# Unread products on TensorE in planned gaps, and a fixed PSUM tile for the second conv

## The chip, the cores and the metric

The kernel runs on one core of one Trainium2 chip. The metric is the device time in microseconds of one execution, from the first to the last instruction of the slowest core (here the only one). Traces come from the hardware profiler; one traced execution is one sample of the same program.

Names used below: TensorE (PE) does matrix products and writes them to PSUM; VectorE (DVE), ScalarE (ACT) and GpSimd (POOL) are the other engines; SyncE (SP) only issues DMAs. "Granted clock" is the share of TensorE's full clock that the throttle let through, as the trace records it.

## The reference

Two layers on an input x of 32 images, 96 channels, 56 x 56 pixels, all float32.

```python
# layer 0: an inverted bottleneck with a residual
h = relu(bn(einsum('oc,bchw->bohw', w1, x)))      # 96 -> 576 channels, the first conv
h = relu(bn(depthwise3x3(h, wdw)))                # 576 channels, 9 taps each
x = x + bn(einsum('oc,bchw->bohw', w2, h))        # 576 -> 96, the second conv

# layer 1, on tokens t = (image, 3136 pixels, 96 channels)
h = relu(bn(einsum('bnc,hc->bnh', layernorm(t), w1)))     # 96 -> 192
X = fft(h, axis=1)                                        # over the 3136 tokens
xr = relu(X.real * rd - X.imag * idg + rb)
xi = relu(X.imag * rd + X.real * idg + ib)
t = t + bn(einsum('bnh,ch->bnc', real(ifft(xr + 1j * xi)), w2))
t = t + ffn(layernorm(t))     # 96 -> 384 -> 96, operands rounded to 8-bit floats, sums to 16-bit
```

The result goes back to the image layout. Batch norms are affine with given statistics, so they fold into weights and biases.

## The kernel before

**Tiling.** An image is done in two halves of 28 rows. The 576 hidden channels are four groups of 128 and one of 64. For each half and each group of 128, `unit` runs the first conv on TensorE (line L584, two products of 406 columns into one PSUM tile `ps`), evicts it on ScalarE with bias and relu (L594, into `hs`), and then does the nine depthwise taps: ScalarE begins the accumulator `acc` (L610) and makes one or two products (L626), VectorE adds six or seven taps (L637), and a DMA of GpSimd adds the products (L645). ScalarE ends with a relu (L654). The last 64 channels go through TensorE instead (`last_channels`: L686, L722, evicted at L705 and L751).

`front` does the second conv (L844, L878, with the residual as transposes of x and the shift as a product with ones at L860) into a PSUM tile of its own, `pw`, in two pieces of four and three groups of 112 pixels, each evicted on ScalarE (L891). It then normalises (L788 to L817), turns the tokens (L945), projects them to 192 (L963) and does the first step of the Fourier transform (L994), whose result goes through DRAM. `mid`, twice per image, does the second step, the weights and relu of the spectrum, the projection back to 96 and the first step of the inverse (L1073, L1102, L1108, L1117, L1159, L1171, L1198 to L1202). `back`, four times per image, does the last step (L1272), the norm, the quantised network (L1289, L1307, L1328, L1340 to L1352, L1369, L1378) and the residual (L1388, L1399, L1404).

Most float32 products stand in the trace as two records each, so a count of 14 is 7 products.

**What sets the order.** Nothing is ordered by hand. Each piece of work is a `Step` with an engine, a cost in microseconds, the steps before it, the buffers that it takes and gives back, and a rank, which says how early it is due. `Plan.emit` plays the whole program through with these costs: whenever an engine falls idle, the ready step of the least rank whose buffers are free is emitted. Each engine's queue is this order, and on the chip each engine works through its queue in order and waits on semaphores where an input isn't there yet. So a gap that the planner sees leaves no trace in the queue: it is just the time until the next instruction's semaphore comes.

The planner has a model of TensorE's throttle in `stretched`: [...]

[...] three `ps` tiles of two banks each, and one `pw` tile of two banks. `pw` is taken from its pool anew for each piece of a half image.

Of the kernel before, what the change touches and what calls it, by code (L numbers as in the profile page):

```python
# [32 lines left out]
F32 = mybir.dt.float32  # L33
# [8 lines left out]
C = 96  # L42
# [86 lines left out]
PACE = {"last": 3.023, "front": 0.4, "mid": 0.54, "back": 0.45}  # L129
CHAIN = 0.6  # L130

OFF = (-4.5, 0.5, 0.5, 8.5)
AT = (3.0, 0.5)

# [14 lines left out]
class Plan:  # L149
# [12 lines left out]
    def __init__(self, free):  # L162
        self.free = dict(free)
        self.steps = []
        self.now = self.pace = 0.0
        self.window, self.share, self.slow = 0, {}, False
        self.moving = []

    def stretched(self, now, work):

        at = now
        while work > 1e-9:
            w = int(at / self.WINDOW + 1e-9)
            while self.window < w:
                x = self.share.pop(self.window, 0.0) / self.WINDOW
                if x < self.LITTLE:
                    self.slow = True
                elif x >= self.FULL:
                    self.slow = False
                self.window += 1  # L180
            rate = 0.5 if self.slow else 1.0
            use = min(work / rate, max((w + 1) * self.WINDOW - at, 1e-6))
            self.share[w] = self.share.get(w, 0.0) + use
            at += use
            work -= use * rate
        return at - now

    def moved(self, now, moves):

# [21 lines left out]
    def emit(self):  # L211
        ready = {s.engine: [] for s in self.steps}
        idle = dict.fromkeys(ready, True)
        for s in self.steps:
            if not s.left:
                heapq.heappush(ready[s.engine], (s.rank, s.at, s))
        events, count, left = [(0.0, 0, None, None)], 1, len(self.steps)
        while events:
            now = events[0][0]
            while events and events[0][0] <= now:  # L220
                _, _, engine, s = heapq.heappop(events)
                if engine:
                    idle[engine] = True
                elif s:
                    for b in s.give:
                        self.free[b] += 1
                    for n in s.next:
                        n.left -= 1
                        if not n.left:
                            heapq.heappush(ready[n.engine], (n.rank, n.at, n))  # L230
            for engine, heap in ready.items():
                if not idle[engine]:
                    continue
                passed, wanted = [], set()
                while heap:
                    item = heapq.heappop(heap)
                    s = item[2]
                    short = {b for b in s.take if self.free[b] < s.take.count(b)}
                    if short or wanted.intersection(s.take):
                        wanted |= short  # L240
                        passed.append(item)
                        continue
                    for b in s.take:
                        self.free[b] -= 1
                    s.emit()
                    left -= 1
                    idle[engine] = False
                    cost = self.stretched(now, s.cost) if engine == "PE" else s.cost
                    late = self.moved(now, s.late) if isinstance(s.late, tuple) else s.late
                    heapq.heappush(events, (now + cost, count, engine, None))  # L250
                    heapq.heappush(events, (now + cost + late, count + 1, None, s))
                    count += 2
                    break
                for item in passed:
                    heapq.heappush(heap, item)
        assert not left, "a step waits for a buffer that nothing frees"


@with_exitstack
def tile_kernel(ctx: ExitStack, tc: tile.TileContext, d: dict, out: bass.AP):  # L260
    nc = tc.nc
# [4 lines left out]
    psa = ctx.enter_context(tc.tile_pool(name="psa", bufs=3, space=PSUM))  # L266
    psw = ctx.enter_context(tc.tile_pool(name="psw", bufs=1, space=PSUM))
    dram = ctx.enter_context(tc.tile_pool(name="scratch", bufs=2, space=DRAM))

    def psum():  # L270
        return psa.tile([128, 2, 512], F32, name="ps", tag="ps")
# [19 lines left out]
    ident = cst([128, 128], "ident")  # L291
# [124 lines left out]
    s = scale_of(vec[:, 0, :], vec[:, 3, :], 128, NK + 1)  # L416

    ps = psum()
    for k in range(NK + 1):
# [3 lines left out]
            lhsT=s[:, k : k + 1].to_broadcast([128, C]),  # L423
            rhs=ident,
            start=True,
            stop=True,
# [4 lines left out]
    s = scale_of(vec[:, 4, :], vec[:, 7, :], 128, NK + 1)  # L431
# [69 lines left out]
    def ffn():  # L501
# [6 lines left out]
        for o, v, p, n in ((b1q, fb, 128, 3), (b2q, fc, C, 1)):  # L508
# [9 lines left out]
    plan = Plan(  # L518
        {
            "ps": 3, "pw": 1, "hs": 3, "acc": 7, "product": 3, "hl0": 1, "hl1": 1, "al": 2,  # L520
            "xt": 1, "norma": 2, "brief": 3, "xnT": 1, "z": 2, "ya": 1, "wb": 1, "yb": 2,
            "V": 2, "eo": 3, "real": 1, "wd": 1, "gd": 1, "tt": 2, "normf": 2, "u8": 1, "uT": 1,
            "h8": 1, "h16": 2, "y16": 1, "ydr": 4, "gdr": 3, "tdr": 4,
        }
    )
# [19 lines left out]
    for n, (f, count) in enumerate(((second, 7), (attention, 6), (mixer, 21), (ffn, 4))):  # L545
        t = step("SP", 0.55 * count, fetch, sets[-1:], late=(150e3, 170e3, 1.5), rank=-20.0 + n)
# [279 lines left out]
    def front(img, s):  # L826

        plan.job(32 * img + 16 * (s + 1) + START["front"], PACE["front"])
        u = {}
        x0 = (R * s - base[s]) * S  # L830

        def conv(i):

            def f():
                if i == 0:
                    if s == 0:

                        ydr[img] = dram.tile([2, NP, S, HA], F32, name="ydr", bufs=4)

                        tdr[img] = dram.tile([2, SK, RP * C], F32, name="tdr", bufs=4)  # L840
                    u["t"] = w1.tile([SK, RP, C], F32, name="xt")

                def add(n, t, src, rhs, rows=slice(None), **k):
                    nc.tensor.matmul(  # L844
                        u["pw"][0:SK, t, n % 4, 0:C],
                        lhsT=src[rows, (G * t + n) * SK : (G * t + n + 1) * SK],
                        rhs=rhs,
                        skip_group_check=True,
                        **k,
                    )  # L850

                if i % 4 == 0:
                    u["pw"] = psw.tile([128, 2, 4, 128], F32, name="pw", tag="pw")
                    n = min(4, G - i)

                    for t in range(2):
                        for m in range(i, i + n):
                            src = xs[img, s][:, x0 : x0 + W]
                            add(m, t, src, ident[0:C, 0:C], start=(m == i), stop=False, is_transpose=True)
                        nc.tensor.matmul(  # L860
                            u["pw"][0:SK, t, 0:n, 0:C],
                            lhsT=ones,
                            rhs=shb[:, 0:n, :],
                            start=False,
                            stop=False,
                            skip_group_check=True,
                        )
                for t in range(2):
                    for k in range(NK):
                        src = acc[img, s, k].rearrange("p r c -> p (r c)")  # L870
                        add(i, t, src, w2T[:, k, :], start=False, stop=False)
                if i in (3, 6):

                    last = acc[img, s, NK].rearrange("p r c -> p (r c)")
                    for n in range(i - i % 4, i + 1):
                        for t in range(2):
                            rows = slice(64 * t, 64 * t + 64)
                            nc.tensor.matmul(  # L878
                                u["pw"][0:SK, t, n % 4, 0:C],
                                lhsT=last[rows, n * SK : (n + 1) * SK],  # L880
                                rhs=w2T[rows, NK, :],
                                start=False,
                                stop=True,
                                skip_group_check=True,
                            )

            return f
# [14 lines left out]
        t = [ready[img, s, k] for k in range(NK)] + [strips[img, s], second_set]  # L902
        ev = []
        for i in range(G):
            n = min(4, G - i) if i % 4 == 0 else 0
            cost = pe(C, SK, 16) + n * (pe(C, SK, 2) + 0.13)
# [12 lines left out]
            if i in (3, 6):  # L919
                a = i - i % 4  # L920
# [498 lines left out]
    for i in range(nimg):  # L1419
        for s in range(2):  # L1420
            load_half(i, s)
            last_channels(i, s)
            for k in range(NK):
                unit(i, s, k)
            front(i, s)
        for half in range(2):
            mid(i, half)
        for h in range(4):
            back(i, h)
    with tc.manual_schedule():  # L1430
        plan.emit()

# [61 lines left out]
```

## Time and profile before

| what | value |
|---|---|
| time, median of 3 runs | 4695.46 us (4678.52 to 4697.34) |
| span of the traced run | 4680.7 us |
| mean granted TensorE clock | 0.967 |
| TensorE busy | 4397.9 us, 94% |
| VectorE busy | 4299.8 us, 92% |
| ScalarE busy | 4170.2 us, 89% |
| taps on VectorE (L637) | 1664 of 1793 ns, 2971.6 us |
| second conv (L844) | 7168 records, 804.9 us |
| eviction of `pw` (L891) | 128 of 629 to 862 ns |

Busy time is the union of an engine's instructions. TensorE's products overlap in its pipeline, so a busy TensorE is not one at its peak, and weight loads stand in a row of their own. The granted clock is given for the whole run and for any stretch. In the rows of waits the numbers are microseconds in total, times, and the longest. The first tap starts at 23.6 us and the last at 4431.3 us. Before and after these there is no depthwise work, and what remains at the end is the chains of the last images' `mid` and `back`.

### The profile page before, as it was taken

The page shows a single profiled execution, that of the slowest core. Times are in us where ns is not written, and L with a number is a line of the kernel's source. Part 1 is how long each engine was busy: PE and PEld are TensorE (multiplying, and loading weights), DVE is VectorE, ACT ScalarE, POOL GpSimd, SP SyncE. Part 2 cuts the span into 40 slices and gives each one's busy share as a digit, 9 for nine tenths or more (in the row PEclk, how much of TensorE's full clock was granted, in tenths as well). Part 3 has the DMA queues.
Part 4 walks back from the last instruction along what each step waited for, and adds up shares of the span by engine and source line. Part 5 has one row for each costly group of instructions (what it writes and reads, how often), then busy time and mean ns, then how long its engine had stood idle before and what let it go on. Part 6 is the DMA issues. An engine that isn't in the chain of part 4 may idle for free.

```text
span 4680.7 us, 85686 instructions
## 1 busy us (share of the span) xinstructions
PE 4397.9 (94%) x33744; PEld 3205.3 (68%) x33744; DVE 4299.8 (92%) x6933; ACT 4170.2 (89%) x5510; POOL 337.3 (7%) x397
## 2 busy tenths in 40 slices
PE   7889999999999999999999999999999999999986
PEld 4567776676676767676777676676776776676774
DVE  8999999999999999999999999999999999999943
ACT  4777999999999999999999999998998999899976
POOL 0000000000000000000000000000000000000000
PEclk7999999999999999999999999999999999999987
DMA  4667777767776767776767777777776776777752
GB/s 97 135 158 172 183 179 171 178 167 171 178 175 166 186 163 185 177 181 167 180 170 176 183 176 169 181 176 171 184 182 166 181 179 163 184 178 175 170 135 78
DMA packets 390887, 789.28 MB, mean 169 GB/s; under 512 B 135600, under 2 KB 236532, under 8 KB 390484
## 3 DMA queue, kind: packets, MB, share of 16 engines
q1 hardware_dynamic: 335028, 479.15, 36.4%
q0 software_dynamic: 55296, 304.64, 33.6%
q8 instruction: 266, 4.36, 0.4%
q14 instruction: 137, 1.12, 0.1%
q10 hardware_dynamic: 160, 0.01, 0.0%
HBM read 286.38 MB, written 192.68 MB: 102 GB/s over the span
## 4 chain that ended last, share of the span: by engine, by line
PE 46%; ACT 14%; DVE 11%; DMA 6%; issue 2%; SPq 0%; POOLq 0%; ACTq 0%; DVEq 0%
PE pw L844 10%; PE ps L584 8%; DVE acc L637 7%; DMA acc<-product 5%; PE ps L722 4%; PE ps L1073 3%; PE ps L994 2%; PE ps L963 2%; PE ps L1369 2%; PE ps L1272 2%; PE ps L1171 2%; ACT acc L654 2%; PE ps L1328 2%; ACT product L626 1%; ACT acc L610 1%
## 5 line engine op out<-in xcount | busy, mean ns | idle before, releaser
L637 DVE SCALAR_TENSOR_TENSOR acc<-hs,wdw,acc 128x1540 f32<-128x1540 f32 (+2 forms) x1664 | 2971.6, 1793 | 27.2 <-ACT acc L610 18.6
L584 PE MATMUL ps<-xs,w1T 96*128 96x406 f32 x2048 | 823.4, 526 | 48.8 <-ACT al L751 11.6
L844 PEld LDWEIGHTS pw<-w2T,acc 128*112 128x112 f32 x7168 | 766.4, 181 | 64.3 <-issue 40.3
L844 PE MATMUL pw<-w2T,acc 128*112 128x96 f32 x7168 | 804.9, 267 | 5.0 <-ACT acc L654 4.8
L626 ACT ACTIVATE product<-hs,wdw 128x1568 f32<-128x1568 f32 (+1 forms) x384 | 609.4, 1591 | 14.5 <-DMA product<-product 14.1
L584 PEld LDWEIGHTS ps<-xs,w1T 96*128 96x128 f32 x2048 | 371.2, 195 | 300.0 <-issue 136.0
L594 ACT ACTIVATE hs<-ps,b 128x812 f32<-128x812 f32 x512 | 478.6, 935 | 97.8 <-PE ps L584 83.2
L645 POOL DMA_DIRECT2D acc<-product x256 | 227.7, 890 | 3306.4 <-DVE acc L637 384.9
L654 ACT ACTIVATE acc<-acc 128x1568 f32<-128x1568 f32 x256 | 386.9, 1512 | 63.8 <-DMA acc<-product 63.5
L610 ACT ACTIVATE acc<-hs,bd,wdw 128x1568 f32<-128x1568 f32 x256 | 435.2, 1700 | 5.5 <-DVE eo L498 5.4
L722 PE MATMUL ps<-hl,band 128*64 128x385 f32 (+3 forms) x3072 | 419.3, 498 | 4.5 <-ACT hs L594 2.3
L963 PE MATMUL ps<-watt,xnT 97*120 97x192 f32 x1792 | 350.3, 341 | 44.3 <-DVE V L1102 31.4
L963 PEld LDWEIGHTS ps<-watt,xnT 97*120 97x120 f32 x1792 | 305.2, 190 | 105.4 <-DVE V L1102 40.2
L1289 ACT ACTIVATE u<-tt,mf,rf 112x96 fp8e5<-112x96 f32 x896 | 346.4, 462 | 6.1 <-DVE mf L820 5.9
L1352 ACT ACTIVATE h<-h 128x784 fp8e5<-128x784 f16 x384 | 329.4, 860 | 22.3 <-DVE h L1346 21.1
L1073 PEld LDWEIGHTS ps<-wb,yb 112*128 112x128 f32 (+1 forms) x3584 | 306.9, 167 | 58.5 <-issue 23.9
L1340 ACT ACTIVATE h<-ps 128x784 f16<-128x784 f32 x384 | 315.4, 824 | 26.8 <-PE ps L1328 25.7
L1073 PE MATMUL ps<-wb,yb 112*128 112x112 f32 (+1 forms) x3584 | 330.7, 273 | 4.0 <-ACT hs L594 1.8
L722 PEld LDWEIGHTS ps<-hl,band 128*64 128x64 f32 (+1 forms) x3072 | 154.7, 135 | 204.1 <-issue 168.8
L1346 DVE TENSOR_SCALAR h<-h,b1q 128x784 f16<-128x784 f16 x384 | 160.8, 419 | 122.0 <-ACT h L1340 119.9
L994 PE MATMUL ps<-z,wa 56*64 56x384 f32 (+1 forms) x2048 | 242.6, 510 | 24.3 <-ACT hs L594 18.2
L1328 PE MATMUL ps<-uT,w1q 96*128 96x392 fp8e5 x768 | 196.9, 341 | 26.5 <-ACT xnT L948 9.5
(148 smaller groups left out, 6395.6 us busy)
## 6 DMA issues: line engine op xcount, KB each, us to landing
acc<-product POOLq DMA_DIRECT2D x256, 784.0 KB, 8.5
product<-product POOLq DMA_DIRECT2D x128, 756.0 KB, 10.7
yb<-ydr SPq DMA_DIRECT2D x256, 294.0 KB
wd<-in_wd_dram SPq DMA_DIRECT2D x128, 349.1 KB
wb<-in_wb_dram SPq DMA_DIRECT2D x64, 686.0 KB
ydr<-ya SPq DMA_DIRECT2D x256, 168.0 KB
xs<-in_x_dram SPq DMA_DIRECT2D x64, 609.0 KB
tdr<-xt SPq DMA_DIRECT2D x64, 588.0 KB
```

What stands on the lines that cost most here:

```text
L584: nc.tensor.matmul(u[h][:, j, 0:QW], lhsT=w1T[:, 128 * k : 128 * (k + 1)], rhs=xs[img, s][0:C, at : at + QW], start=True, stop=True,)
L594: nc.scalar.activation(flat[:, 2 * h * QW : 2 * (h + 1) * QW].rearrange("p (j w) -> p j w", j=2), u[h][:, :, 0:QW], AF.Relu, bias=b1[:, k ...
L610: nc.scalar.activation(acc[img, s, k], u["hs"][:, o + up : o + up + R, :], AF.Identity, scale=weight(up, 0), bias=bd[:, k : k + 1],)
L626: nc.scalar.activation(u["p", dr][:, ra:rb, :], u["hs"][:, ra + o + dr : rb + o + dr, :], AF.Copy, scale=weight(dr, 0))
L637: nc.vector.scalar_tensor_tensor(dst, src, weight(dr, dc), dst, ALU.mult, ALU.add)
L654: nc.scalar.activation(acc[img, s, k], acc[img, s, k], AF.Relu)
L722: nc.tensor.matmul(pv[:, :, ca:cb], lhsT=band[rows, j, dc + 1, 64 * o : 64 * o + 64], rhs=H[rows, q : q + 7, ca + dc : cb + dc], skip_grou ...
L844: nc.tensor.matmul(u["pw"][0:SK, t, n % 4, 0:C], lhsT=src[rows, (G * t + n) * SK : (G * t + n + 1) * SK], rhs=rhs, skip_group_check=True, **k,
L963: nc.tensor.matmul(pv[0:PK, q - a, 0:HA], lhsT=xnT[:, q, 0:PK], rhs=watt, start=True, stop=True,)
L994: nc.tensor.matmul(u["y", b][64 * c : 64 * c + n, j, 0 : 2 * HA], lhsT=wa[at, 0:n], rhs=rhs, start=True, stop=True)
L1073: nc.tensor.matmul(o, lhsT=lhsT, rhs=u["wb"][:, G * s + q, :], start=True, stop=True)
L1289: nc.scalar.activation(u["u8"][:, q, :], u["t"][:, q, :], AF.Identity, scale=u["r"][:, q : q + 1], bias=u["m"][:, q : q + 1], saturate=False,)
```

## The change

It does two things.

Where the planner finds TensorE idle with no step that it could start, and TensorE was used for less than three quarters (`SPARSE`) of the last window, it now emits a filler: a product of the 128 x 128 identity with itself, which nothing reads, for which the planner's clock moves on by 0.23 us (`FILLER`). When the planned filler ends, the planner looks again. Fillers stop when no TensorE step is left. [...]

For a place to put the filler's result, the `pw` tile becomes one fixed tile of two banks for the whole kernel. Its slots are 96 columns wide in place of 128, so that four of them leave the last 128 columns of each bank free; the filler writes into those of the first bank. One product before the plan opens the accumulation there.

```diff
--- before.py
+++ after.py
@@ -129,6 +129,9 @@
 PACE = {"last": 3.023, "front": 0.4, "mid": 0.54, "back": 0.45}
 CHAIN = 0.6
 
+SPARSE = 0.75
+FILLER = 0.23
+
 OFF = (-4.5, 0.5, 0.5, 8.5)
 AT = (3.0, 0.5)
 
@@ -165,6 +168,7 @@
         self.now = self.pace = 0.0
         self.window, self.share, self.slow = 0, {}, False
         self.moving = []
+        self.filler, self.recent = None, []
 
     def stretched(self, now, work):
 
@@ -185,6 +189,11 @@
             work -= use * rate
         return at - now
 
+    def sparse(self, now):
+
+        self.recent = [r for r in self.recent if r[1] > now - self.WINDOW]
+        return sum(b - max(a, now - self.WINDOW) for a, b in self.recent) < SPARSE * self.WINDOW
+
     def moved(self, now, moves):
 
         size, rate, extra = moves
@@ -215,6 +224,7 @@
             if not s.left:
                 heapq.heappush(ready[s.engine], (s.rank, s.at, s))
         events, count, left = [(0.0, 0, None, None)], 1, len(self.steps)
+        work = sum(s.engine == "PE" for s in self.steps)
         while events:
             now = events[0][0]
             while events and events[0][0] <= now:
@@ -246,6 +256,9 @@
                     left -= 1
                     idle[engine] = False
                     cost = self.stretched(now, s.cost) if engine == "PE" else s.cost
+                    if engine == "PE":
+                        self.recent.append((now, now + cost))
+                        work -= 1
                     late = self.moved(now, s.late) if isinstance(s.late, tuple) else s.late
                     heapq.heappush(events, (now + cost, count, engine, None))
                     heapq.heappush(events, (now + cost + late, count + 1, None, s))
@@ -253,6 +266,14 @@
                     break
                 for item in passed:
                     heapq.heappush(heap, item)
+                if engine == "PE" and idle[engine] and work and now > 0 and self.sparse(now):
+
+                    self.filler()
+                    idle[engine] = False
+                    cost = self.stretched(now, FILLER)
+                    self.recent.append((now, now + cost))
+                    heapq.heappush(events, (now + cost, count, engine, None))
+                    count += 1
         assert not left, "a step waits for a buffer that nothing frees"
 
 
@@ -266,6 +287,9 @@
     psa = ctx.enter_context(tc.tile_pool(name="psa", bufs=3, space=PSUM))
     psw = ctx.enter_context(tc.tile_pool(name="psw", bufs=1, space=PSUM))
     dram = ctx.enter_context(tc.tile_pool(name="scratch", bufs=2, space=DRAM))
+
+
+    pw = psw.tile([128, 2, 512], F32, name="pw", tag="pw")
 
     def psum():
         return psa.tile([128, 2, 512], F32, name="ps", tag="ps")
@@ -850,7 +874,7 @@
                     )
 
                 if i % 4 == 0:
-                    u["pw"] = psw.tile([128, 2, 4, 128], F32, name="pw", tag="pw")
+                    u["pw"] = pw[:, :, 0 : 4 * C].rearrange("p t (q c) -> p t q c", c=C)
                     n = min(4, G - i)
 
                     for t in range(2):
@@ -1427,6 +1451,12 @@
             mid(i, half)
         for h in range(4):
             back(i, h)
+
+    def filler():
+        nc.tensor.matmul(pw[:, 0, 4 * C :], lhsT=ident, rhs=ident, start=False, stop=False, skip_group_check=True)
+
+    nc.tensor.matmul(pw[:, 0, 4 * C :], lhsT=ident, rhs=ident, start=True, stop=False, skip_group_check=True)
+    plan.filler = filler
     with tc.manual_schedule():
         plan.emit()
```

## The prediction

> **What bounds the kernel now.** I read the page first for the shares of the engines, then the table of windows for three stages (start, steady state, end), then the chain of waits over the end, and last who waited for whom on TensorE. The page's parts 1 and 4:
>
> ```profile
> PE 4397.9 (94%) x33744; PEld 3205.3 (68%) x33744; DVE 4299.8 (92%) x6933; ACT 4170.2 (89%) x5510; POOL 337.3 (7%) x397
> ...
> PE 46%; ACT 14%; DVE 11%; DMA 6%; issue 2%; SPq 0%; POOLq 0%; ACTq 0%; DVEq 0%
> ```
>
> Three engines are each busy for about nine tenths of 4681 us, and TensorE has the largest part of the chain. No single engine can be named from this; the stages differ. The windows (busy us of PE, weight loads, DVE, ACT, POOL, then the granted TensorE clock and the DMA columns):
>
> ```profile
> 0.00:530.00 530.00, 454.37 (x3075) 318.84 (x3076) 484.04 (x613) 381.55 (x428) 45.76 (x63) 0.89 0.64 144
> 530.00:4430.00 3900.00, 3754.36 (x29375) 2739.06 (x29374) 3710.06 (x5971) 3610.98 (x4784) 290.71 (x334) 0.99 0.73 176
> 4430.00:4680.00 250.00, 189.18 (x1295) 147.42 (x1294) 105.66 (x351) 177.71 (x300) 0.86 (x1) 0.80 0.42 110
> ```
>
> The start is VectorE's (484 of 530 us busy), with a TensorE clock of 0.89. In the steady state TensorE is 96% busy, VectorE 95%, ScalarE 93%, and the clock is almost whole. In the last 250 us the depthwise taps are over: no engine is full, one image's chain runs after another, and the clock is 0.80. A low clock costs most where the chain is bare. The chain of waits over the end shows the same work twice (start us, us, what):
>
> ```profile
> 4559.13 1.38 PE ps L1272 x14
> ...
> 4616.07 2.60 PE ps L1272 x14
> ...
> 4652.60 2.69 PE ps L1272 x14
> ```
>
> and the windows beside two of them:
>
> ```profile
> 4480.00:4490.00 10.00, 6.04 (x60) 4.83 (x60) 6.51 (x13) 8.58 (x18) 0.00 (x0) 0.94 0.35 107
> 4490.00:4495.00 5.00, 4.75 (x21) 4.56 (x19) 2.91 (x4) 3.20 (x4) 0.00 (x0) 0.50 0.08 29
> ...
> 4650.00:4655.00 5.00, 4.70 (x21) 3.65 (x22) 0.00 (x0) 3.04 (x8) 0.00 (x0) 0.50 0.23 69
> ```
>
> A group of 7 products costs 1.38 us at the whole clock and 2.69 us where the granted clock is 0.50; a stretch in which TensorE was busy 6.04 of 10 us was enough to lose it.
>
> [...] 2.69 / 1.38 = 1.95, and the granted clock is 0.50 in the stretch. [...] between 4478 and 4492 the longest wait of TensorE was 2.5 us (line L945 for DVE xn L937), and the clock fell all the same. [...]
>
> **The change, part by part.** *Number and place of fillers.* The built instruction order has 961 fillers and one opening product, in 300 runs: 217 lie among the first four images' first-conv products (L584), 487 among those of the other 28, 257 after the last one. Apart from them, each engine has as many instructions as before, but the planner's interleaving has shifted everywhere, since a filler holds the planned TensorE for 0.23 us.
>
> *Price of one.* The trace has no warm 128x128 by 128 f32 product alone. From below: L1171, 7 products of 128x112 weights and 96 columns, takes 1.54 us on the chain (at 4472), 0.22 us each. From above: that times 128/112, 0.25 us. [...] I take 0.23: 50 us of TensorE at the start, 112 in the steady state, 59 at the end, 221 in all.
>
> *Clock lost before.* The mean clock is 0.967, so 0.033 x 4681 = 154 us of full clock were lost: 0.11 x 530 = 58 at the start, 0.20 x 250 = 50 at the end, and about 46 in the steady state.
>
> *Start.* VectorE idles 46 us of 530; about 8 of them lie in the first 20 us of loading and setup. The other 38 are dips at image borders, where TensorE has a burst of second conv and attention products to do and begins it at half clock after a gap. The 58 us can't return more than those 38. I take 15: ScalarE and DMA waits share the dips. Filler time costs nothing here, as TensorE idles 76 us (530 - 454) against 50 us of fillers.
>
> *Steady state.* The order puts the fillers once per image beside L963, L994, L1328, L1388 and L1307, 12 and 22 of them in alternate images. In the trace of before TensorE's waits there in this stage were
>
> ```profile
> PE ps L963 <- DVE V L1102: 31.4, 25, 2.6
> PE ps L994 <- ACT hs L594: 18.2, 20, 2.4
> PE ps L1328 <- ACT xnT L948: 9.5, 6, 2.2
> PE ps L1328 <- ACT z L976: 7.2, 2, 3.7
> PE ps L1388 <- DVE V L1102: 7.1, 10, 1.4
> ```
>
> 73 us, with L584 after ACT z (5.4) 79 us of the 146 that TensorE idles. So 112 - 79 = 33 us of fillers have no idle time to lie in and stand in front of real products, whose evictions (L594, L976) and taps queue behind them. Against that stand 46 us of lost clock, of which I count 0.6 on the path, the part that TensorE has in a chain nearly covered by engines (46 of 79%): 29 us. Net +4 us.
>
> *End.* I went down the chain from 4434 and took from each cold piece its warm twin: L963 twice 4.8 against 2.3, L1272 three times 2.6 to 2.7 against 1.38, L1159 three times 2.9 against 1.55, L1388 and L1369 some 0.5 too long each time. The excess comes to about 22 us. The fillers raise use from 181 of 240 us (some of it stretched) by 59 us, [...] I count nine tenths kept, 20 us. Some 30 runs lie on the chain and a product that becomes ready meets a running filler, half of 0.23 us each: 3.5 us back. Net -16.5.
>
> *The PSUM tile.* One fixed tile in place of one per half image, slots of 96 in place of 128: same bytes evicted, same number of products; the next conv waits for L891's eviction as it did. Three of the 961 fillers newly wait for ScalarE. Behind such a filler all of TensorE is queued. L844's longest wait for ACT xt was 1.8 us, so at most 5.4 us in all; hidden for the most part, as the filler stood in a gap: 0, upper bound 5.
>
> Sum: 4695.5 - 15 + 4 - 16.5 = **4668 us**.
>
> **The rivals.** *TensorE becomes the bound.* In the steady state the planned gaps need not be gaps on the chip: an order that is late on TensorE executes the fillers anyway, at once and without a wait. If half of the 79 us are met, 72 us of fillers displace work; with half of the 46 us recovered that is +49, with -6 at the start and -10 at the end: 4728 us. For it: 96% busy already, 146 us spare against 112 of fillers. Against: VectorE and ScalarE are as full, so a late TensorE is partly absorbed. *The clock isn't held.* Nothing paces the fillers on the chip: a run goes off back to back at the front of a gap and leaves the rest empty, [...]. Then a third of the gains at the ends (-10) and half the displacement (+5): 4690 us. For it: waits of 3.8 us in the end (L1369 for ACT h). *All of it returns.* Fillers lie in idle time alone, start -25, end -19, steady state -15: 4636 us.
>
> **How the numbers follow.** Forecast 0.48, TensorE bound 0.24, clock not held 0.18, all returns 0.10. The forecast spreads over some 15 us to each side, by the reordering alone; the bound of 0.5% is 4672 below and 4719 above. Faster: 0.30 of the forecast, 0.10, and 0.02 of "not held", 0.42. Slower: 0.21 of the TensorE case and 0.02 of the others, 0.23. Same: the remaining 0.35. Range 4636 to 4728: the two outer cases' times, which leave half of each outside, about 0.17; the price bounds of a filler (0.22 to 0.25) move the steady state by -5 to +10 and lie inside.
>
> **What would show it.** Right: the clock over the last 250 us above 0.9 and L1272 at 1.4 us throughout; the start's clock above 0.95, with fewer VectorE dips; 3900 us of steady state within 10 us. Wrong: a steady state longer by 20 us or more with TensorE above 98% busy (first rival); a clock in the end that stays near 0.8 with fillers in short bunches before idle time (second rival); or a time that moves while the clock does not, which would put it on the new interleaving.

## The result, and the profile after

The kernel after takes 4662.5 us (median of 4 runs, 4660.0 to 4665.7), the kernel before 4695.5 (median of 4, 4678.5 to 4697.3). The ratio of the means is 0.9938 with a 95% interval of 0.9914 to 0.9962: faster by 0.6%. The forecast was 4668.

The page of after, busy time by engine and the chain of waits by engine:

```profile
PE 4507.9 (97%) x35666; PEld 3363.0 (72%) x35666; DVE 4297.8 (92%) x6933; ACT 4177.0 (90%) x5510; POOL 339.8 (7%) x397
...
PE 60%; ACT 13%; DVE 13%; issue 3%; DMA 3%; SPq 0%; DVEq 0%; ACTq 0%; POOLq 0%
```

The chain of waits could be followed back to 360 us here and only to 928 us in before, and its shares are of the whole span. So TensorE's 60% here and 46% there don't compare as they stand.

TensorE has 1922 more records (two to a filler and to the opening product, 962 products; two records are missing) and is busy 110 us longer, in a span that is 22.5 us shorter. The same three windows as before (PE, weight loads, DVE, ACT, POOL, then the clock and the DMA columns):

```profile
0.00:530.00 530.00, 477.01 (x3432) 348.95 (x3432) 466.58 (x599) 367.53 (x409) 44.83 (x61) 0.94 0.63 141
530.00:4430.00 3900.00, 3828.37 (x30511) 2839.69 (x30511) 3734.05 (x6000) 3646.19 (x4826) 295.00 (x336) 1.00 0.74 177
4430.00:4658.00 228.00, 202.49 (x1725) 174.38 (x1724) 97.20 (x335) 163.25 (x279) 0.00 (x0) 0.97 0.41 111
```

The clock rose in all three: 0.89 to 0.94, 0.99 to 1.00, 0.80 to 0.97. In the start VectorE did less, not more: 466.6 us against 484.0. And the group of seven products that cost 2.6 to 2.7 us in the cold stretches of the end (clock 0.50; now line L1296) costs 1.38 to 1.63 us wherever the chain of waits has it after 4425 us, and 1.38 in its last five places, of which three are:

```profile
4580.11 1.38 PE ps L1296 x14
...
4607.24 1.38 PE ps L1296 x14
...
4634.27 1.38 PE ps L1296 x14
```

The waits of TensorE in the steady state (530 to 4430 us; total, times, longest):

```profile
PE ps L1412 <- DVE V L1126: 14.3, 25, 0.9
PE ps L1393 <- ACT xnT L972: 12.8, 12, 1.1
PE ps L987 <- DVE V L1126: 11.3, 16, 1.3
```

L987 is L963 of before, which waited 31.4 us there; 11.3 are left.

To see where the time went I cut each trace at three events instead of fixed times: the first depthwise tap, the 209th (image 5 begins; 52 taps to an image) and the last of 1664. All in us of the traced run, with "clock lost" as (1 - granted clock) times the stretch:

| | first tap | image 5 begins | image 5 to last tap | last tap to end | clock lost: start, middle, end |
|---|---|---|---|---|---|
| before | 23.6 | 508.7 | 3922.6 | 249.4 | 56, 46, 51 |
| after | 36.0 | 525.7 | 3885.1 | 247.3 | 31, 0, 8 |

The start got 17 us longer, the middle 37.5 us shorter, the end only 2 us shorter. The middle and the end of before, as the trace gives them (those of after stand below, beside the same order without fillers):

```profile
508.70:4431.30 3922.60, 3774.19 (x29517) 2754.36 (x29515) 3732.16 (x5993) 3633.33 (x4815) 293.08 (x336) 0.99 0.73 175
4431.30:4680.70 249.40, 188.23 (x1291) 146.81 (x1289) 104.36 (x350) 176.41 (x298) 0.86 (x1) 0.79 0.42 110
```

These are single traced runs; the kernel with the tile alone (below), whose order is that of before, has a middle of 3932.2 and an end of 247.0, so such numbers scatter by some 10 us in the middle and 2 in the end where the clock isn't held.

### The profile page after: what moved, and what is told of

Read it like the earlier page. It is cut to its first block, busy times and chain, and to the rows that moved or that the text cites. A ratio compares the mean times of both kernels' runs of the same rounds, so it can differ in the third digit from the quotient of the medians.

```text
span 4658.2 us, 89512 instructions
## 1 busy us (share of the span) xinstructions
PE 4507.9 (97%) x35666; PEld 3363.0 (72%) x35666; DVE 4297.8 (92%) x6933; ACT 4177.0 (90%) x5510; POOL 339.8 (7%) x397
## 4 chain that ended last, share of the span: by engine, by line
PE 60%; ACT 13%; DVE 13%; issue 3%; DMA 3%; SPq 0%; DVEq 0%; ACTq 0%; POOLq 0%
PE pw L868 15%; PE ps L608 10%; DVE acc L661 7%; PE ps L1097 4%; PE ps L1018 4%; PE ps L987 3%; PE ps L1296 3%; ACT product L650 2%; PE ps L1195 2%; PE ps L1352 2%; PE ps L746 2%; PE pw L902 2%; PE ps L710 2%; PE ps L1393 2%; PE ps L1183 2%
## 5 line engine op out<-in xcount | busy, mean ns | idle before, releaser
L608 PE MATMUL ps<-xs,w1T 96*128 96x406 f32 x2048 | 806.0, 516 | 18.4 <-ACT hs L618 13.5
L868 PEld LDWEIGHTS pw<-w2T,acc 128*112 128x112 f32 x7168 | 752.2, 179 | 64.7 <-issue 44.6
L650 ACT ACTIVATE product<-hs,wdw 128x1568 f32<-128x1568 f32 (+1 forms) x384 | 609.5, 1588 | 17.1 <-DMA product<-product 16.7
L987 PE MATMUL ps<-watt,xnT 97*120 97x192 f32 x1792 | 336.0, 331 | 15.0 <-DVE V L1126 12.3
L987 PEld LDWEIGHTS ps<-watt,xnT 97*120 97x120 f32 x1792 | 294.2, 184 | 69.7 <-issue 36.2
L1456 PE MATMUL pw<-ident 128*128 128x128 f32 x1920 | 276.8, 283 | 3.2 <-ACT xt L915 3.2
L1456 PEld LDWEIGHTS pw<-ident 128*128 128x128 f32 x1920 | 254.5, 196 | 25.8 <-issue 12.8
```

The lines of the kernel that those rows point to most:

```text
L608: nc.tensor.matmul(u[h][:, j, 0:QW], lhsT=w1T[:, 128 * k : 128 * (k + 1)], rhs=xs[img, s][0:C, at : at + QW], start=True, stop=True,)
L650: nc.scalar.activation(u["p", dr][:, ra:rb, :], u["hs"][:, ra + o + dr : rb + o + dr, :], AF.Copy, scale=weight(dr, 0))
L868: nc.tensor.matmul(u["pw"][0:SK, t, n % 4, 0:C], lhsT=src[rows, (G * t + n) * SK : (G * t + n + 1) * SK], rhs=rhs, skip_group_check=True, **k,
L987: nc.tensor.matmul(pv[0:PK, q - a, 0:HA], lhsT=xnT[:, q, 0:PK], rhs=watt, start=True, stop=True,)
L1456: nc.tensor.matmul(pw[:, 0, 4 * C :], lhsT=ident, rhs=ident, start=False, stop=False, skip_group_check=True)
```

## The experiments

Two theories. **The clock**: the fillers hold TensorE's clock, and that is the gain. **The interleaving**: a filler takes time in the plan, so every queue has a new order; the order is the gain, or part of it.

Edits are shown in part: `...` stands for what is left out, notes after `#` are mine, and `calls` counts the fillers that the plan has asked for.

**Planned, not emitted (e1).** The new order without one filler.

```diff
     def filler():
-        nc.tensor.matmul(pw[:, 0, 4 * C :], lhsT=ident, ...)
+        pass
```

> The order of after on every engine, with the fillers planned but not put into the queue. Theory 1 (the clock): the fillers hold the granted clock, and the gain in the steady state is theirs. Then the clock falls back to about 0.96 to 0.97, the depthwise stage (first tap to last tap, 4375 us in after, 4408 in before) grows back to 4395 or more, and the whole is 4680 to 4700 us. Theory 2 (the interleaving): the gain is the new order's, and fillers only cost. Then the stage stays at 4375 or shrinks, and the whole is 4640 to 4660 us although the clock is low.

Measured: 4707.0 us, ratio 1.0024 (1.0012 to 1.0036), a little over what theory 1 expected. Clock 0.962, clock lost 67, 58 and 53 us by stage. Its middle and end by its own events, and under them those of after:

```profile
528.30:4444.60 3916.30, 3784.78 (x29470) 2757.18 (x29469) 3732.29 (x5986) 3637.51 (x4805) 293.49 (x336) 0.99 0.74 175
4444.60:4699.50 254.90, 191.34 (x1334) 147.52 (x1332) 107.59 (x355) 178.94 (x303) 0.86 (x1) 0.79 0.42 111
```

```profile
525.70:4410.90 3885.20, 3818.08 (x30425) 2830.74 (x30424) 3727.88 (x5987) 3635.58 (x4805) 295.01 (x336) 1.00 0.74 177
4410.90:4658.20 247.30, 217.09 (x1847) 187.49 (x1844) 107.67 (x355) 178.16 (x303) 0.86 (x1) 0.97 0.43 115
```

The order alone is slower than before, by 0.2%. It costs most in the start: the first tap comes at 29.2 us and image 5 begins at 528.3, against 23.6 and 508.7. With the same order on every engine, the fillers take 31 us off the middle and 7.6 off the end. Theory 2 falls as the source of the gain; the order is a cost.

**The tile alone (e2).** Before, with one fixed `pw` and slots of 96, no fillers.

```diff
-                    u["pw"] = psw.tile([128, 2, 4, 128], F32, name="pw", tag="pw")
+                    u["pw"] = pw[:, :, 0 : 4 * C].rearrange("p t (q c) -> p t q c", c=C)
```

> The kernel before with only the fixed PSUM tile and slots of 96; no fillers, the same order on every engine. Both theories: no change, 4690 to 4700 us (ratio 0.997 to 1.003). If the tile were worth something, its eviction (629 to 862 ns in before) or the conv's waits would move and the ratio would be under 0.997.

Measured: 4694.5 us, ratio 1.0002 (0.9989 to 1.0015). The tile is worth nothing by itself, as forecast.

**The order of before, with fillers (e5).** In before's plan, with the fixed tile, ahead of each TensorE step, as many fillers as fit the planned gap less 0.85 us; they take no time in the plan.

```diff
+                    if engine == "PE":
+                        for _ in range(int(max(0.0, now - self.ended - 0.85) / 0.23)):
+                            self.filler()
                     s.emit()
```

> The order of before on every engine, with fillers put into the gaps that its own plan has on TensorE (as many as fill the gap less 0.85 us, at 0.23 us each: 553, of which 229 in the first four images, 161 in the others, 164 after the last first conv); they take no time in the plan. Fixed tile as in after. Theory 1 (the clock): clock 0.98 or more, depthwise stage 4380 to 4395 us, whole 4660 to 4680. Theory 2 (the interleaving): stage 4400 to 4420 us, whole 4690 to 4710 us although the clock rises.

Measured: 4671.5 us, ratio 0.9954 (0.9938 to 0.9971), clock 0.987. With the old order on every engine the fillers alone are a gain of 0.5%. Its 161 fillers in the middle left 20 us of clock lost there and the middle at 3914.3 us, 8 to 18 us under the two traces of this order without fillers, which themselves differ by 10 (I expected 4380 to 4395 us from first to last tap; it was 4404). The start got 4.5 us longer (image 5 begins at 513.2 us). The end is where it won:

```profile
4427.50:4662.90 235.40, 196.49 (x1619) 165.54 (x1617) 104.39 (x350) 175.12 (x298) 0.86 (x1) 0.95 0.44 117
```

235 us against 249 in before and 247 in after. So theory 1 holds on both orders, and the order of after has a worse end.

**The first 24 fillers (e3).** After, without the fillers that stand ahead of the first conv.

```diff
+        calls.append(0)
+        if len(calls) > 24:
             nc.tensor.matmul(...)
```

> The order of after, without the first 24 fillers alone, which stand ahead of the first conv and take 6.9 us there. In after the first tap starts at 36.0 us, in before at 23.6. If the time of these fillers makes the delay, the first tap comes at 24 to 29 us and the whole at 4650 to 4656. If it is the order that the plan made with them (the second norm's square root behind the first eviction on ScalarE, and its copies behind later loads), the first tap stays at 31 us or later, and the whole at 4657 to 4663.

Measured: 4653.0 us, ratio 0.9919 (0.9903 to 0.9935), first tap at 29.3 us: 6.7 of the 12.4 us of delay returned. Both causes are at work: the order without a filler has its first tap at 29.2 us, so 5.6 us of the delay are the order's and the rest is the 24 fillers'. The timelines show how. TensorE and then ScalarE in after (start us, us, engine, line, operation; in brackets the idle time before and what ended it):

```profile
7.83 6.86 PE L1456 MATMUL pw<-ident 128*128 128x128 f32 x48
14.53 5.63 PE L608 MATMUL ps<-xs,w1T 96*128 96x406 f32 x16
```

```profile
16.10 0.94 ACT L618 ACTIVATE hs<-ps,b 128x812 f32<-128x812 f32 x1 [11.97 <-PE ps L608]
16.94 0.27 ACT L430 ACTIVATE V<-V 128x96 f32<-128x96 f32 x1
30.09 2.35 ACTq L482 DMA_DIRECT2D shb<-yb  x3
32.49 1.77 ACT L618 ACTIVATE hs<-ps,b 128x812 f32<-128x812 f32 x2 [15.28 <-DMA shb<-yb]
```

and ScalarE in before:

```profile
10.85 0.28 ACT L406 ACTIVATE V<-V 128x96 f32<-128x96 f32 x1 [6.62 <-DVE V L405]
14.06 5.09 ACTq L458 DMA_DIRECT2D shb<-yb  x3
19.20 2.59 ACT L594 ACTIVATE hs<-ps,b 128x812 f32<-128x812 f32 x3 [8.07 <-DMA shb<-yb]
```

24 fillers take 6.9 us there, 0.29 us each against 0.23 in the plan, and the first conv starts at 14.5 instead of 9.2 us. Since the new plan put one eviction ahead of the square root (L430) on ScalarE, the square root waits too, then VectorE's second norm, then the copies of the shift (L482), and behind these in ScalarE's queue all other evictions. In the run without the 24 the order keeps its defect: the other evictions come at 25.8 us, and the profile names a load (`yb<-in_a_b_dram`) as what ended ScalarE's wait there. That in after, too, an earlier load held the copies back until 30.1 us, though VectorE had their data ready at 21.7, is inferred from this.

This run also prices the other fillers of the start, since the planned but not emitted order has its first tap at the same time. From the first tap to image 5, without and with them:

```profile
29.20:528.30 499.10, 430.38 (x2915) 296.33 (x2915) 450.69 (x544) 357.39 (x395) 42.05 (x48) 0.87 0.63 142
29.30:519.70 490.40, 455.29 (x3321) 331.01 (x3321) 450.55 (x544) 357.04 (x395) 41.22 (x48) 0.95 0.64 145
```

On this order they are worth some 9 us (after and its variants e6 and e7, which have them too, take 489.3 to 491.2), and they don't make up for what the order costs: before needs 485.1 us for the same stretch.

**No filler in the first 40 us of the plan (e8).**

```diff
-                if engine == "PE" and idle[engine] and work and now > 0 and self.sparse(now):
+                if engine == "PE" and idle[engine] and work and now > 40 and self.sparse(now):
```

> The planner as in after, but no filler in the first 40 us of its plan (900 fillers in place of 961). ScalarE's first rows then stand as in before: square root and copies ahead of the first eviction. If the start is lost by what the fillers do to the plan there, the first tap comes at 23 to 24 us (36.0 in after) and the whole at 4646 to 4654 us. If the first images take up such a delay in any case, the whole stays at 4657 to 4665.

Measured: 4643.8 us, ratio 0.9895 (0.9875 to 0.9915); first tap 23.4 us, image 5 begins at 508.4. The start's whole loss is returned, and no more: it is that of before (508.7), although the clock lost there is 29 us against 56. The whole time is a little under the 4646 to 4654 us that I expected.

**The price of a filler in the middle (e6 twice, e7 half).** The order of after; 487 planned fillers put in twice (974 in all; the 973 and 486 of the expectation are one too few), or every second one left out.

```diff
+        for _ in range(2 if 217 < len(calls) <= 704 else 1):                  # twice
+        for _ in range(len(calls) % 2 if 217 < len(calls) <= 704 else 1):     # half
             nc.tensor.matmul(...)
```

> The order of after, but each of the 487 fillers among the first convs of images 5 to 32 is put in twice (973 of them); the plan knows of one. It prices a filler there. If fillers stand in front of real products (the prediction's 33 us for 487), 486 more, some 110 us of TensorE, lengthen the stage from 3885 us to 3960 or more and the whole to 4735 or more. If they lie in time in which TensorE waits anyhow (67 us were left idle in after), the first 67 us cost little: stage 3900 to 3930, whole 4675 to 4710.

> The same order, with every second one of those 487 fillers left out (243 stay). If the number matters because the clock needs it, the clock lost in this stage (0 us in after, 58 without fillers) comes back in part, 15 to 35 us, and the stage is 3892 to 3905 us, the whole 4668 to 4682. If half is enough and the rest only costs, the stage is 3870 to 3883 and the whole 4648 to 4660.

Measured: twice 4710.9 us, ratio 1.0034 (1.0021 to 1.0048); half 4654.1 us, ratio 0.9916 (0.9899 to 0.9934). The middles, twice and then half:

```profile
526.80:4462.50 3935.70, 3901.95 (x31382) 2937.69 (x31380) 3728.39 (x5987) 3646.06 (x4805) 293.87 (x335) 1.00 0.74 175
```

```profile
525.40:4405.20 3879.80, 3786.45 (x29947) 2780.91 (x29945) 3731.66 (x5986) 3635.11 (x4805) 294.91 (x336) 1.00 0.74 177
```

By number of fillers in the middle: 0 gives 3916 us, 243 give 3880, 487 give 3885, 974 give 3936. The first 243 hold the clock (3.4 us lost). The next 244 cost 5 us here and 8.5 on the order of e8 (below), 0.02 to 0.03 each. That is little but not chance: the six traced runs with all 487 have middles of 3885.1 to 3889.2 us, the three with half 3879.0 to 3879.8, and the whole time fell by 8 us both times. The last 487 cost 50.5 us, 0.10 each, where TensorE's idle time in the stage has shrunk from 67 to 34 us. A filler was cheap while TensorE's gaps could take it. My range for "twice" (3900 to 3930) was just missed.

**The end (e9, e11, e12).** First, in e9, the plan of e8 up to the last first conv, and then fillers that take no time in the plan, as in e5.

```diff
-        work = sum(s.engine == "PE" for s in self.steps)
+        work = sum(s.emit.__name__ == "mm" for s in self.steps)    # first convs left
...
+                    if engine == "PE" and not work:
+                        for _ in range(int(max(0.0, now - self.ended - 0.85) / 0.23)):
+                            self.filler()
```

> As e8, and after the last first conv the planner takes no time for fillers; it puts into its gaps as many as fill them less 0.85 us (160 in place of 245 to 257), as e5 did for its whole run. The end (last tap to last instruction) was 249 us in before, 247 in after, 235 in e5. If after's end gains little because planned fillers hold back the chain and change its order, the end here is 233 to 240 us and the whole 4633 to 4643. If it is luck of the order alone, the end is 245 to 255 us and the whole as e8.

Measured: 4646.7 us, ratio 0.9905 (0.9885 to 0.9924); end 251.3 us. That idea fell: e5's short end isn't had by taking the fillers' time out of the plan. The run changes two things, though: the end has 160 fillers in place of 245, and a clock of 0.92 (20 us lost), so what planned time alone does on this order isn't shown. Then the plan of e8 with half, and with none, of the end's fillers:

```diff
+        if len(calls) % 2 or len(calls) <= 655:     # half
+        if len(calls) <= 655:                       # none
             nc.tensor.matmul(...)
```

> The plan of e8 with every second filler after the last first conv left out (123 of 245 stay). If the end is held back by fillers on its chain, it shortens from 245 us to 235 to 241. If they only hold the clock, the clock lost there rises from 5 us to 15 to 30 and the end is 246 to 252. If neither counts, since other engines and transfers set the end in this order: 243 to 247 either way.

> The plan of e8 with no filler after the last first conv. The clock lost in the end should be about 50 us, as in before. If the clock is worth there what the prediction gave it (20 us of chain, less 3.5 us that fillers cost), the end is 260 us or longer. If transfers and ScalarE take over the chain where TensorE is fast, it is 247 to 255.

Measured: half 4649.9 us, ratio 0.9899 (0.9883 to 0.9916); none 4659.8, ratio 0.9918 (0.9903 to 0.9933). The ends of none, half and all (e8):

```profile
4400.60:4662.20 261.60, 196.23 (x1334) 152.91 (x1332) 107.63 (x355) 179.67 (x303) 0.86 (x1) 0.78 0.41 109
```

```profile
4394.70:4646.90 252.20, 203.06 (x1579) 169.70 (x1577) 107.61 (x356) 178.70 (x303) 0.86 (x1) 0.90 0.43 113
```

```profile
4396.20:4641.50 245.30, 212.76 (x1823) 183.84 (x1821) 107.69 (x355) 178.59 (x303) 0.86 (x1) 0.98 0.44 116
```

262, 252, 245 us at clocks of 0.78, 0.90, 0.98: on one order, the end follows the clock, and the fillers are worth 16.3 us net. Here half is not enough.

**Both gains, and the start alone (e10, e13).** e8 with every second filler of the middle left out; then also without the start's 168.

```diff
+        if len(calls) % 2 or not 168 < len(calls) <= 655:                       # half the middle
             nc.tensor.matmul(...)
...
+        if len(calls) > 168 and (len(calls) % 2 or len(calls) > 655):           # and no start
             nc.tensor.matmul(...)
```

> Both gains together: the plan of e8 (no filler in its first 40 us) with every second filler of the middle left out, as in e7. If the two are independent: start as e8 (image 5 begins at 508 us), middle 3880 to 3885, whole 4636 to 4641 us, against 4643.8 of e8. If e7's 8 us were chance of its runs: 4642 to 4648.

> The order of e10, with the 168 fillers among the first four images' first convs left out as well. It prices the start alone. Image 5 begins at 508.2 us in e10 and 508.7 in before. If the clock lost in the start (56 us in before, 31 in e10) lies beside VectorE's work and costs nothing, image 5 begins at 505 to 512 us and the whole is 4633 to 4642. If the fillers recover what the prediction gave them (15 us), image 5 begins at 518 us or later and the whole is 4648 or more.

Measured: 4636.0 us, ratio 0.987 (0.9855 to 0.9884), and 4638.2, ratio 0.9889 (0.9868 to 0.9911). The first has the lowest median of all. Their runs overlap (4634.3 to 4639.5 us and 4635.3 to 4646.6), and both beat both kernels. From the first tap to image 5, with and without the start's fillers:

```profile
23.40:508.20 484.80, 452.12 (x3265) 326.80 (x3264) 451.22 (x543) 356.59 (x396) 40.74 (x47) 0.94 0.65 147
```

```profile
23.60:510.00 486.40, 427.68 (x2926) 296.68 (x2925) 451.06 (x542) 356.38 (x395) 40.74 (x47) 0.88 0.65 146
```

A clock of 0.94 against 0.88 is worth about 2 us there, which is within the scatter. VectorE needs 451 us of the stretch either way.

## Why the prediction was right, and where its steps were wrong

The time lay within the range and the direction was right, but that the sum came within 6 us is luck, since its errors cancel: forecast -15, +4, -16.5 by stage; traced +17, -37.5, -2.

- **Start, -15: wrong in both its halves.** The step that failed is the claim that filler time costs nothing because TensorE idles 76 us. It idles, but the first fillers stood ahead of the first conv, and the plan moved ScalarE's queue around them: 12.4 us on the first tap, of which 6.7 came back without the 24 fillers, and all in e8, whose plan has no filler in its first 40 us. The new order, which the sum has no term for, also costs 14 us from the first tap to image 5 (499.1 against 485.1, without fillers). And the gain was small: some 9 us on the order of after, about 2 on that of e8, where the clock lost lay beside VectorE's taps (busy 451 of 485 us). The bursts did run cold, as I had said: in before, for one, TensorE was busy 1.32 of the 3.4 us to 447.5, and then the clock was 0.50 for 10.3 us. I had named VectorE as the bound and then counted a gain from TensorE all the same.
- **Middle, the clock term: right in size.** I counted 0.6 of the lost clock on the path, 29 of 46 us (0.6 of 46 is 28, a slip of 1). On one order, 58 us of lost clock came back and the stage shrank by 31 us, a share of 0.54 with the fillers' own cost inside; with half the fillers 54 came back for 36.5 us, a share of 0.67.
- **Middle, displacement +33 us: mis-sized.** Measured: 5 to 8.5 us for the second half of the 487. The cost of the first half can't be told apart from the clock's gain, with which it comes. The step compared 112 us of fillers with the idle time of *another order* and only beside the products that the fillers neighbour. On after's own order without fillers TensorE idles 131.5 us in this stage, and 67 are left with them, which agrees with fillers that lie in gaps. The mechanism is real: it appears with 974 fillers, at 0.10 us each.
- **End, -16.5: right for the fillers on one order, wrong for the change.** Fillers on a fixed order are worth 16.3 us (order of e8), 7.6 (after) and 12 to 14 (before: 247 to 249 against 235). That nine tenths of the clock would be kept was an estimate: the clock lost there went from 51 us to 8, so 0.84 came back. What the forecast left out is the new interleaving, which costs 5.5 us there without fillers (254.9 against 249.4), and 12 in the order of e8 (261.6). Summing the chain's pieces from the last tap on by engine, before has no DMA wait in it (PE 129.6 us, ACT 69.1). The order of after has 12.1 us of DMA waits without fillers and 17.8 with them, while TensorE falls from 103 to 84 us; the order of before with fillers (e5) has 4.3. Why this order brings those waits onto the chain I haven't tested.
- **The tile, 0: right** (ratio 1.0002, 0.9989 to 1.0015).
- **The rivals.** "TensorE becomes the bound" did not happen with 487 fillers and did with 974 (4710.9 us; TensorE idle 34 of 3936 us). "The clock isn't held" didn't happen. "All of it returns" is near what e10 reaches (4636 forecast, 4636.0 measured), but not by its route: against before the start gave nothing, the middle 43 us and the end 4.
- **The signs that I had set** held in part. The end's clock is over 0.9 (0.97), and L1296 came near 1.4 us but not throughout (up to 1.63). The other two failed: the start's clock is 0.94, not over 0.95, with less VectorE work done (466.6 against 484.0 us), and the steady state is 37.5 us shorter, not the same within 10. So the signs spoke against the steps although the time came out. The start's clock rose and its time got worse: a clock is not a time.

## What to carry to other kernels

A product that nobody reads, put where TensorE had a gap, bought clock here (0.962 without the fillers, 0.992 with them, on the order of after), and the clock was time where TensorE was on the chain: in the middle (31 us) and the end (7.6 to 16.3 us), and less so in the start (9 and 2 us), where VectorE sets the pace (451 of 485 us busy in e10). Put no filler ahead of the first real work (24 of them delayed the first tap by 6.7 us), and use as few as hold the clock; here half of them did in a stage 96% busy (3.4 us of clock lost), and all were needed in the sparse end (a clock of 0.90 with half, 0.98 with all). When a planner decides the order, an instruction that takes planned time is two changes, so run the new order without the instruction, and the instruction in the old order.

## What the runs showed of the hardware that I had not expected

- Eight fillers (128x128 by 128 columns, f32) in a row took 1.79 us on after's chain (from 4620.45 us) at a clock of 1.00, 0.22 us each; the plan takes 0.23. In the middle 487 more of them (e6) added 84 us of busy time, 0.17 each, and 50.5 us to the stage. Why these add less than 0.22 each isn't shown.
- The mean use of a stretch did not tell its clock. In after, TensorE was busy 17.5 of 22 us from 4405 to 4427 us at a clock of 1.00, with 8.0 us of the chain waiting for one DMA addition (`acc<-product`, from 4416), and then the clock was 0.50 for 13.6 us. The last 3.4 us before the fall, and the stretch behind it:

```profile
4424.10:4427.50 3.40, 1.07 (x9) 1.07 (x10) 0.80 (x3) 3.34 (x4) 0.00 (x0) 1.00 0.46 142
4427.50:4441.10 13.60, 13.60 (x63) 10.87 (x62) 5.13 (x9) 5.87 (x9) 0.00 (x0) 0.50 0.42 97
```

TensorE was busy 0.31 of those 3.4 us, with a longest wait of 2.67 us. I cut before's trace into pieces of 3.41 us, the length of the shortest of its clock records, from the edges of these records. After 4441 us its clock fell to 0.50 eleven times, for 6.8 to 17.1 us, each time after a piece in which TensorE was busy 0.12 to 0.57 of the time, and stayed at 1.00 after every piece of 0.65 or more. No sharp limit is shown: in the rest of before the clock fell after pieces of up to 0.72 and stayed after some down to 0.56. With half the end's fillers (e11) TensorE was busy 203 of 252 us, and a tenth of the clock was still lost (0.90).

- Three of the 961 fillers waited for the eviction of `pw`, 3.2 us in all (longest 1.4): the bound of 5 us held.
